# Layers 2 and 3 of a fused four-layer network: TensorE changes between them after every second pair of tiles

## The chip, the cores and the metric

The kernel runs on one core of a Trainium2 chip. The metric is the device time of one execution in microseconds (us), from the launch of the program on the core to its end. Five engines have instruction queues of their own: PE (TensorE, matrix multiplication), DVE (VectorE), ACT (ScalarE), POOL (GpSimd) and SP (SyncE, here only a queue that issues DMAs). PE writes its results to PSUM; DVE and ACT move them from there to SBUF, which is called an eviction below.

## The reference, cut to what matters

The input x is (4, 8, 512, 512) in f32; its first axis is called t below (0 to 3). Four layers follow, each of the form x = x + layer(gn(x)), where gn normalises every group of two channels over the whole image. Layer 0 is an attention with spiking neurons, layer 1 a 13 x 13 convolution of each channel. The change touches layers 2 and 3, two 3 x 3 convolutions over the 8 channels:

```python
def layer2(x):                       # x already normalised
    sx, sw = 127 / max(abs(x)), 127 / max(abs(weight))
    qx, qw = clip(round(x * sx)), clip(round(weight * sw))
    return conv3x3(qx, qw) / (sx * sw) + bias
def layer3(x):
    return conv3x3(x, weight) + bias
x = x + layer2(gn(x))
x = x + layer3(gn(x))                # this is the output
```

Layer 3 of one t can't start before the statistics of that t after layer 2 are known, since gn needs the mean and the variance of the whole image.

## The kernel before, in words

Layers 0 and 1 run first and leave x in DRAM, one tensor `x2` for each t. Function `layers23` then runs layers 2 and 3 in one loop.

**Tiles and pairs.** The 512 rows of an image are cut into 85 windows of 8 rows, each 6 rows after the last. A window has 8 rows x 8 channels = 64 partitions, so a tile of 128 partitions holds two windows, and two tiles make a pair. Each t has 22 pairs (`N_PAIRS`); the last of them holds a single window. A convolution is a matrix product with a banded matrix over the partitions, done three times with shifted columns. Layer 2 multiplies a whole tile by a 128 x 128 matrix in bf16, three matmuls for a tile, six for a pair (line L1118). Layer 3 works in f32 on each window alone, in one of four 64 x 64 quarters of the array, four quarters at a time: 24 matmuls for a pair (L1221).

**One turn of the loop.** Turn n issues layer 2 of pair n, counted over all t, and layer 3 of the pair 25 turns behind (22 pairs of a t and `LAG` = 3). In the order of the program it does this:

- `load` of pair n+5: two DMAs on SP bring x from DRAM into a tile of the pool `early["x"]` (L1068). The pool has 9 such tiles.
- `normalise` of pair n+2: ACT writes y (L1085; pool of 2). `quantise` of pair n+1: DVE rounds y to bf16 into one of three buffers xq (L1097), and POOL copies its two border columns (L1101, L1102).
- `layer2` of pair n: for each of its two tiles three matmuls on PE into a PSUM tile of the pool `ps_2`, called ps_q, which has 3; then DVE's eviction (L1125), which adds x and writes the sum into the ring `x3` in SBUF. For the statistics either ACT squares the tile and sums it (L1132) or DVE takes bn_stats (L1137).
- `halos`: where windows overlap, DMAs copy rows between neighbours in the ring (L1276), on SP's queue for t = 0 and on POOL's afterwards.
- `layer3` of pair n-25: POOL writes the border columns (L1214), PE multiplies into two PSUM tiles of `ps_3` (called ps_r, 4 tiles), ACT evicts them to o (L1230, pool of 10), and SP issues two DMAs to the output (L1237).
- Two steps of `norm3`, a generator that starts after the last pair of a t and computes its mean, variance and scaled band matrix. It is a chain of short DVE instructions (L1172 to L1203 and L178 to L197) with two small matmuls of line L181, the first for the mean and the second for the variance, and one of line L1199.

So turns 0 to 24 have layer 2 alone, turns 25 to 87 both layers, and turns 88 to 112 layer 3 alone. The first of a t's pairs has index 0, 22, 44 or 66.

**What sets the order.** Each engine runs its queue in order. The queues are laid out before the run by a scheduler that follows the order of the program and the dependences, and may move an instruction ahead of others where it expects time. `tc.issue_after(op)` keeps a block's instructions behind `op` on the same engine. PSUM tiles, tiles of x and the ring are reused in turn, and an instruction that writes a reused one waits for its last reader.

The ring `x3` has `RING` = 26 places of a pair. Pair n takes the place of pair n-26, whose layer 3 was issued in turn n-1. The lines that the change touches are these:

```python
HALF = P // 2
LAG = 3
RING = 23 + LAG
...
        "x": ctx.enter_context(pool("x2", 9, side="right")),
...
        if n >= N_PAIRS + LAG:
            t, p = divmod(n - N_PAIRS - LAG, N_PAIRS)
            with tc.issue_after(did):
                behind = (layer3(t, p, *norms[t]),)
```

## Time and profile before

| what | value |
|---|---|
| median of 3 runs | 2920.96 us (2919.23 to 2924.84) |
| profiled execution, its own time | 2921.53 us |
| its span, first to last instruction | 2919.3 us |
| TensorE clock granted, mean | 0.990 |
| layers 2 and 3, from about 2514 us to the end | 405 us |
| of these, both layers together | 2588 to 2849 us |
| PE busy over the span | 2819.7 us (97%) |
| DVE, ACT, POOL busy over the span | 2208.5, 551.0, 888.1 us |

The profile records one execution. A row of its views gives a source line, an engine, an operation, the tensors written and read, how often, and a time; times in the timeline count from the start of the span. In brackets stands how long the engine was idle before and what ended the wait. L1118 is line 1118 of the kernel before. The chain of waits is followed back from the last instruction to whatever released it each time; a line on it is on the path that sets the end.

### The profile page before, as it was taken

Reading aid. Unit: us, or ns where it says so; the run is one execution under the profiler, and the core shown is the slowest. Engines: PE = TensorE matmul, PEld = TensorE weight load, DVE = VectorE, ACT = ScalarE, POOL = GpSimd, SP = SyncE. Lnnn points to the kernel's source line nnn. Section 1 sums busy time; section 2 is a strip of 40 time slices with the busy share of each in tenths; the row PEclk is TensorE's granted clock in tenths of the full one; section 3 lists DMA queues with packets and bytes.
Section 4 is the critical chain, followed back from the end, with each engine's and each line's share of the span. In section 5 each row is a group of like instructions: output and inputs, shape, how many; then the busy total and the mean of one; then the engine's idle time right before and its main releaser. Section 6 shows DMA issues by size and latency. Waiting matters only on the chain. (4 is left out here: it accounts for less than half of the span.)

```text
span 2919.3 us, 36593 instructions
## 1 busy us (share of the span) xinstructions
PE 2819.7 (97%) x12865; PEld 1301.8 (45%) x12865; DVE 2208.5 (76%) x3916; ACT 551.0 (19%) x860; POOL 888.1 (30%) x1928
## 2 busy tenths in 40 slices
PE   6899999999999999999999999999999999679999
PEld 3454455554555554455455555545333333223334
DVE  7898688688779868877886886796665566888870
ACT  1300010010010001001000100110111121677774
POOL 3243233334224333323432343332311111232220
PEclk9899999999999999999999999999999999999999
DMA  7332322222322222222222111112877778699975
GB/s 180 96 81 78 79 62 63 70 70 77 73 59 66 69 75 74 69 59 67 69 70 59 45 52 52 52 52 62 226 202 207 201 212 220 170 199 238 219 193 147
DMA packets 323895, 322.10 MB, mean 110 GB/s; under 512 B 21431, under 2 KB 237183, under 8 KB 323599
## 3 DMA queue, kind: packets, MB, share of 16 engines
q1 hardware_dynamic: 261872, 237.39, 33.4%
q0 software_dynamic: 19776, 56.14, 6.0%
q10 hardware_dynamic: 42063, 26.23, 3.2%
q8 instruction: 101, 1.65, 0.3%
q14 instruction: 83, 0.68, 0.1%
HBM read 210.57 MB, written 103.60 MB: 108 GB/s over the span
## 5 line engine op out<-in xcount | busy, mean ns | idle before, releaser
L499 PE MATMUL ps_in<-w_v,xn 128*128 128x512 f32 x1024 | 459.5, 599 | 3.0 <-DVE xn L480 3.0
L499 PE MATMUL ps_in<-w_kq,xn 128*128 128x512 f32 x1024 | 450.1, 592 | 0.0
L815 PE MATMUL ps_conv<-x,bt 112*64 112x512 f32 x2048 | 445.2, 592 | 0.8 <-DVE v_p L467 0.8
L499 PE MATMUL ps_in<-xn,w_kq 128*128 128x512 f32 x1024 | 444.6, 592 | 0.0
L535 PE MATMUL ps_b<-toep,vtok 128*64 128x512 bf16 x3072 | 368.2, 383 | 1.0 <-DVE v_o L550 1.0
L450 ACT ACTIVATE h_q<-v_q,c_half 128x512 f32<-128x512 f32 x96 | 69.2, 721 | 1473.1 <-DVE v_q L446 852.3
L475 POOL TENSOR_TENSOR h_v<-h_v,c_v 128x512 f32<-128x512 f32 x96 | 121.9, 1270 | 686.0 <-DVE h_v L474 660.0
L584 POOL COPY x1s<-x1s 128x2 f32<-128x2 f32 (+1 forms) x1024 | 227.7, 277 | 273.3 <-DVE x1s L573 273.3
L562 PE MATMUL ps_out<-wp,so 128*128 128x512 f32 x1024 | 308.9, 444 | 0.0
L499 PEld LDWEIGHTS ps_in<-xn,w_kq 128*128 128x128 f32 x1024 | 194.3, 190 | 233.0 <-issue 222.0
L499 PEld LDWEIGHTS ps_in<-w_kq,xn 128*128 128x128 f32 x1024 | 194.2, 190 | 219.9 <-issue 205.0
L499 PEld LDWEIGHTS ps_in<-w_v,xn 128*128 128x128 f32 x1024 | 191.0, 191 | 218.5 <-issue 210.2
L815 PEld LDWEIGHTS ps_conv<-x,bt 112*64 112x64 f32 x2048 | 146.4, 135 | 288.9 <-issue 286.5
L535 PEld LDWEIGHTS <-vtok 128*64 128x64 bf16 x3072 | 175.6, 111 | 154.7 <-issue 5.6
L1221 PE MATMUL ps_conv<-x,band_t 64*64 64x512 f32 x2040 | 242.6, 595 | 0.0
L562 PEld LDWEIGHTS ps_out<-wp,so 128*128 128x128 f32 x1024 | 192.6, 188 | 94.4 <-issue 57.8
L1125 DVE SCALAR_TENSOR_TENSOR x<-ps_conv,inv,x 128x512 f32<-128x512 f32 (+1 forms) x172 | 187.4, 1185 | 45.7 <-PE ps_conv L1118 45.6
L573 DVE SCALAR_TENSOR_TENSOR x1s<-v_p,xr 128x256 f32<-128x256 f32 x256 | 188.5, 776 | 14.9 <-DMA x<-x1s 4.1
L837 POOL DMA_DIRECT2D x<-xo x128 | 71.6, 566 | 330.8 <-ACT xo L822 316.4
L822 ACT ACTIVATE xo<-ps_conv,off 128x512 f32<-128x512 f32 x128 | 87.8, 688 | 431.1 <-PE ps_conv L815 310.2
L475 POOL TENSOR_TENSOR h_k<-h_k,c_k 128x512 f32<-128x512 f32 x96 | 123.2, 1284 | 134.0 <-DVE h_k L474 134.0
L1118 PE MATMUL ps_conv<-xq,band 128*128 128x512 bf16 (+1 forms) x516 | 132.2, 393 | 30.3 <-POOL xq L1101 30.3
(193 smaller groups left out, 3161.4 us busy)
## 6 DMA issues: line engine op xcount, KB each, us to landing
x<-x SPq DMA_DIRECT2D x64, 917.0 KB
x<-x SPq DMA_DIRECT2D x168, 256.0 KB
x<-x1s POOLq DMA_DIRECT2D x128, 262.0 KB, 2.6
xq<-in_x SPq DMA_DIRECT2D x128, 256.0 KB
xr<-in_x SPq DMA_DIRECT2D x128, 256.0 KB
out<-o SPq DMA_DIRECT2D x164, 192.0 KB
xs<-in_x SPq DMA_DIRECT2D x112, 256.0 KB
x<-xo ACTq DMA_DIRECT2D x128, 128.0 KB
```

The source lines that it names most:

```text
L475: nc.gpsimd.tensor_add(h, h, c_twice[n])
L499: mm = nc.tensor.matmul(ps, lhsT=lhsT, rhs=rhs, start=k == 0, stop=k == NC - 1)
L535: nc.tensor.matmul(pb[two * DH : (two + 1) * DH, :], lhsT=v[:, c, h * DH : (h + 1) * DH], rhs=toep[z][:, h, u : u + N], start=c == 0 and z ...
L562: nc.tensor.matmul(ps, lhsT=so[:, k, c * P : (c + 1) * P], rhs=wpT[z][:, k, :], start=k == 0 and z == 0, stop=k == NC - 1 and z == 1,)
L573: nc.vector.scalar_tensor_tensor(own, v.rearrange("p (g v) -> p g v", g=PH)[:, two, :], 1.0, by_phase[:, two, :], op0=ALU.is_ge, op1=ALU.add,)
L584: nc.gpsimd.tensor_copy(x1[:, f, u : u + n], x1[:, fm, um - n + 1 : um + 1][:, ::-1])
L815: mm = nc.tensor.matmul(ps[q * M1 : (q + 1) * M1, :], lhsT=bt[:, z, :], rhs=xt[:, w0 : w0 + N_PS1, z : z + NV], start=z == 0, stop=z == SH ...
L822: nc.scalar.activation(xo[:, a, :], ps, AF.Identity, bias=off[:, t : t + 1])
L837: engine.dma_start(bass.AP(dst.tensor, dst.offset + (q * n_half * W1_OUT * B + b) * D + f * NV, [[B * D, W1_OUT], [W1_OUT * B * D, n_half] ...
L1118: mm = nc.tensor.matmul(ps[:n_p, :], lhsT=w["band2"][:n_p, j, dx, :n_p], rhs=xq[:, j, dx : dx + PH, :], start=dx == 0, stop=dx == 2,)
L1125: done["DVE"] = nc.vector.scalar_tensor_tensor(own.rearrange("p (v g) -> p g v", g=PH), by_phase(ps[:n_p, :]), w["inv"][:n_p], by_phase(x[ ...
L1221: mm = nc.tensor.matmul(ps[j][b * HALF : (b + 1) * HALF, :], lhsT=band[half, b, dx, :], rhs=x3[half, s0 + j, dx : dx + D], start=dx == 0, ...
```

## The change

Layer 3 is no longer issued in every turn. Its pairs are collected in the list `due`, and in turns with an odd n, and in every turn after the last of layer 2, all that is due is issued. So an even turn issues layer 2 of one pair and no layer 3, and an odd turn issues layer 2 of one pair and then layer 3 of two. Turn 25 still issues one.

Since layer 3 of a pair may come one turn later, the ring gets one more place, 27. A place holds 2 x 514 f32 numbers in each partition (4112 bytes), a tile of the pool of x 2 x 512 (4096 bytes); the pool of x goes from 9 tiles to 8.

```diff
-RING = 23 + LAG
+RING = 24 + LAG
...
-        "x": ctx.enter_context(pool("x2", 9, side="right")),
+        "x": ctx.enter_context(pool("x2", 8, side="right")),
...
-    norms, norm, done, behind = {}, iter(()), {}, ()
+    norms, norm, done, behind, due = {}, iter(()), {}, (), []
...
         if n >= N_PAIRS + LAG:
-            t, p = divmod(n - N_PAIRS - LAG, N_PAIRS)
+            due.append(divmod(n - N_PAIRS - LAG, N_PAIRS))
+        if due and (n % 2 or n >= n_all):
             with tc.issue_after(did):
-                behind = (layer3(t, p, *norms[t]),)
+                for t, p in due:
+                    behind = (layer3(t, p, *norms[t]),)
+            due = []
```

## The prediction

> **What bounds the kernel now.** I read the table by stage first, to see which engine fills each stretch of layers 2 and 3, then the chain of waits for what ends last, then the order of time around one turn. The stretches here are a mixed one (layers 2 and 3 together) and the tail (layer 3 alone); the columns are length, busy time of PE, weight loads, DVE, ACT and POOL, then PE clock, DMA share and GB/s.

> ```profile
> 2688.80:2745.00 56.20, 56.20 (x415) 18.01 (x414) 45.03 (x70) 41.69 (x70) 15.80 (x42) 1.00 0.92 245
> 2858.00:2910.00 52.00, 52.00 (x492) 27.41 (x488) 0.16 (x1) 27.84 (x41) 1.16 (x9) 1.00 0.54 159
> ```

> PE is never idle in either; DVE is at 80%, ACT 74%, DMA 92% in the mixed stretch. The chain agrees (start, length, what):

> ```profile
> 2692.96 2.74 PE ps_conv L1221 x24
> 2695.70 1.40 PE ps_conv L1118 x6
> 2697.09 2.74 PE ps_conv L1221 x24
> ...
> 2749.48 0.77 PE ps_conv L1118 x3
> ```

> A turn costs 1.40 + 2.74 = 4.14 us, all PE. How much of it is matmul? Three matmuls of L1118 end in 0.77 and six in 1.40, so one more costs 0.21. In the tail, where L1221 runs alone, ACT's evictions of a pair follow each other at 2898.52, 2901.09, 2903.67: 2.57 us for the same 24 matmuls. These run four at a time, so a step is 2.57/6 = 0.43[...]. Pure work is 6 x 0.214 + 2.57 = 3.86. The other **0.28 us is the two switches** between the layers: about 0.11 from 2 to 3, and 2.74 - 2.57 = 0.17 back.

> ```profile
> 2898.52 1.51 ACT L1230 ACTIVATE o<-ps_conv,const 128x512 f32<-128x512 f32 x2 [1.06 <-PE ps_conv L1221]
> 2901.09 1.51 ACT L1230 ACTIVATE o<-ps_conv,const 128x512 f32<-128x512 f32 x2 [1.06 <-PE ps_conv L1221]
> ```

> Where t changes, DVE is the bound for six turns: it also does norm3 there, and PE waits for it (timeline of PE):

> ```profile
> 2664.70 1.47 PE L1118 MATMUL ps_conv<-xq,band 128*128 128x512 bf16 x6
> 2666.83 0.38 PE L181 MATMUL gps_x<-gsum_x,avg_same 128*128 128x1 f32 x2 [0.66 <-DVE gsum_x L178]
> 2667.14 2.81 PE L1221 MATMUL ps_conv<-x,band_t 64*64 64x512 f32 x24
> 2669.88 1.47 PE L1118 MATMUL ps_conv<-xq,band 128*128 128x512 bf16 x6
> 2671.59 0.38 PE L181 MATMUL gps_x<-gsum_x,avg_same 128*128 128x1 f32 x2 [0.24 <-DVE gsum_x L178]
> ```

> Between the two L181 (the mean, then the variance) lies a pair of layer 3, which covers DVE's chain from one to the other: PE waits 0.66 + 0.24 only.

> [...]

> **The change part by part.**

> *Switches.* Turns 25 to 87 hold both layers: 63 times there and back now. Afterwards turn 25, then the odd turns 27 to 87: 32. The built program's order shows it (layer 2 of an even turn and an odd one, then two pairs of layer 3). At most 31 x 0.28 = 8.7 us go.

> *A new wait for PSUM.* Two pairs of layer 2 on end need four tiles, and ps_q has three. In the trace layer 2 begins at 2703.90 and DVE's first eviction at 2704.76, 0.86 later:

> ```profile
> 2703.90 1.47 PE L1118 MATMUL ps_conv<-xq,band 128*128 128x512 bf16 x6
> ...
> 2704.76 2.14 DVE L1125 SCALAR_TENSOR_TENSOR x<-ps_conv,inv,x 128x512 f32<-128x512 f32 x2 [0.86 <-PE ps_conv L1118]
> ```

> One eviction takes about 1.15 (1.109 is the least, 1.177 the mean of the group in 2700 to 2750). With 0.05 to hand over (gsum_x ends 2576.35, PE starts 2576.40) the bank is free at 0.86 + 1.15 + 0.05 = 2.06; PE wants it after three tiles, 3 x 0.643 = 1.93. It waits **0.13**, with all of layer 3 queued behind. Two turns become 2.06 + 0.64 + 0.11 + 5.14 + 0.17 = 8.13, instead of 8.28: 0.15 gained. The bounds are no wait (DVE's evictions start 0.99 apart; gain 0.28) and a wait that eats the switch (gain 0). Undisturbed doubles are turns 28 to 41, 48 to 63, 70 to 85: 7 + 8 + 8 = 23. **-3.4 us** (0 to -6.5).

> *DVE, ACT and POOL within a double.* DVE needs 2 x 3.27 (2704.76 to 2708.03, next idle) = 6.5 of 8.1. The odd turn's quantise ends near 7.4 and POOL's two copies (0.4 each) near 8.3; PE asks at 9.4: covered. ACT now does square, y, square, y, then four o: it resumes with square 2 near 6.3 and is done near 10.9, where the next square is just due; the next pair of layer 3 needs its banks at 10.8, and they were freed at 9.7. Cost 0, with some 1 us of cover.

> *The start.* Turn 27's layer 2 now follows turn 26's at once. Its quantise starts at 2592.14 and the first POOL copy ends at 2593.36 in the trace; PE would be free at 2591.00 + 1.29 = 2592.29. It waits 1.1, and gets back the 0.28 of a switch: **+0.8**.

> *Where t changes (turns 42 to 47 and 64 to 69).* Now 2657.36 to 2683.21 = 25.85 us. In the new order only layer 2 of turn 45 lies between the mean's L181 and the next layer 3, and the variance's L181 sits late in that pair. On DVE gsum_x now stands behind both evictions, bn_stats and the quantise of turn 45. Laid out from turn 42 (0): PE 1.29 + 0.64 + 0.11 + 5.14 + 0.17 reaches turn 44 at 7.35. DVE evicts 42 from 0.86, and with one more eviction and the norm's first part (2661.43 to 2663.42 is 1.99, 2665.79 to 2666.69 is 0.90) is free for turn 44 near 9.1. Two evictions 1.97, bn_stats 0.61, mean 0.1, quantise 0.6, two more evictions 1.97, bn_stats 0.61, quantise 0.6 and the five short norm steps (about 1.1) put gsum_x at 16.7. PE stands at that L181 from 13.2: **a wait of about 3.5 instead of 0.9**. Then 0.3 + 3.1 + 0.17 to turn 46, two pairs of layer 2 with the last norm matmul 3.0, layer 3 5.25 and 0.17: turn 48 near 28.7. Each of the two costs 2.8: **+5.6**. Bounds 1.5 each (the short steps fully overlapped, evictions 0.97) and 4 each[...].

> *The end.* Turns 86 and 87 keep their L181 wait (0.36) and save one switch: **-0.3**.

> *Queues and pools.* SP issues four output DMAs, then four loads, instead of two and two: 8 per 8.1 us as before. A load waits for its tile of x to be evicted, eight pairs back instead of nine: issued near 14 within the double, needed past 30. In turns 0 to 22 it loses one turn of lead (2.6 us) out of six; near 2547 SP is held up to 1.3 us by it, while the load issued at 2558.13 lands 8.91 later, 3.8 before its y. Cost 0, up to 1.3. POOL's halo DMAs keep their number but for the ring's wrap. The ring of 27 keeps the reuse one turn behind layer 3, as now: 0. Layers 0 and 1 are untouched.

> *Sum.* -3.4 + 0.8 + 5.6 - 0.3 = **+2.7** on the profiled execution's 2921.53. That execution is 0.6 above the median of the runs, 2920.96; against the median: 2923.7 us.

> **Rivals.** *Full gain:* all 31 switches go and nothing waits: -8.7, 2912.3. For it: PE is the only full engine between the changes of t. Against: three banks, and DVE's order at the changes of t. *The PSUM wait eats the gain:* if DVE begins an eviction later than 0.86, or a stopped PE restarts slowly, the fourth tile waits 0.28 or more; from there the doubles give nothing, and the start and the changes of t stand: +6.1, 2927; at 0.4 per double it is 2930. For it: DVE has 20% to spare only. Against: DVE is idle 0.86 before each first eviction now. *DMA:* the share is 0.92 to 0.95 already, and bunched output could make loads late; 257 GB/s were moved in 2596.6 to 2655, and 8.13 us need 1.96 MB, 241 GB/s, so I expect none; each us lost per double would cost 23. *It does nothing:* excluded by the built order.

> **Numbers.** A measurement of this kernel tells about 0.2% (5.8 us) from no change. Likeliest case, within that, 0.60; it holds the lost half of the switches and the longer norm wait in every size named above. Slower, by the PSUM wait or the DMA queue, 0.28. Faster, the full gain, 0.12. Range: 2917.5 (no PSUM wait and 1.5 per change of t: -3.1 - 2.6 from the sum, less a little) to 2931 (no gain in the doubles, 4 per change of t, 1.3 of late loads).

> **What would show it.** Right: L1118 in runs of 12 and L1221 in runs of 48; doubles of about 8.13 us, with a small wait of L1118 for DVE's L1125; one wait of 3 to 4 us at each of the two variance L181; 28 to 29 us over turns 42 to 47. Wrong: doubles of 8.0 without a wait, or of 8.28 and more; no long L181 wait; ACT or PE waiting for DMA in the mixed stretch.

## The result, and the profile after

| | before | after |
|---|---|---|
| median of 6 runs each | 2920.98 us (2919.23 to 2924.84) | 2936.81 us (2930.61 to 2939.81) |
| profiled execution, its own time | 2921.53 us | 2934.12 us |
| its span | 2919.3 us | 2932.3 us |

The ratio is 1.0051, with a 95% interval of 1.0041 to 1.0061: the change costs 12 to 18 us. The forecast of 2923.7 us, with a range up to 2931.0, was wrong. The runs of after also lie wider apart (9.2 us) than those of before (5.6).

Most of what was forecast is in the profile. A *double* is an even turn and the odd turn after it: two pairs of layer 2, then two of layer 3. In the table by stage (columns as in the prediction), the mixed stretch and the tail are as full as before:

```profile
2702.70:2759.60 56.90, 56.87 (x424) 19.76 (x420) 45.08 (x70) 41.74 (x68) 14.45 (x36) 1.00 0.89 217
2870.00:2922.00 52.00, 52.00 (x491) 20.53 (x488) 0.00 (x0) 27.06 (x40) 0.00 (x0) 1.00 0.51 150
```

In the chain of waits of after, L1118 comes in runs of 12 and L1221 in runs of 48, and one double follows the other at 2710.93 and 2719.07, 8.14 us apart. The timeline has their starts 8.13 apart (2710.87 and 2719.00), the forecast to the last digit; two turns cost 8.28 before.

```profile
2710.93 2.82 PE ps_conv L1118 x12
2713.75 5.32 PE ps_conv L1221 x48
2719.07 2.80 PE ps_conv L1118 x12
```

Where t changes, the timeline of PE has the forecast's one long wait, at the variance's L181:

```profile
2674.49 2.79 PE L1221 MATMUL ps_conv<-x,band_t 64*64 64x512 f32 x18
2679.95 0.38 PE L181 MATMUL gps_x<-gsum_x,avg_same 128*128 128x1 f32 x2 [2.68 <-DVE gsum_x L178]
2680.27 3.66 PE L1221 MATMUL ps_conv<-x,band_t 64*64 64x512 f32 x30
```

It is 2.68 us where 3.5 was laid out, and turns 42 to 47 take 27.82 us (2664.34 to 2692.16) where 28.7 was laid out.

What was not forecast stands in the view of waits. These are PE's waits from 2585 to 2905 us by line (us in total, times, longest), first before, then after:

```profile
PE gps_x L181 <- DVE gsum_x L178: 2.1, 5, 0.7
PE ps_conv L1118 <- POOL xq L1101: 1.4, 1, 1.4
```

```profile
PE ps_conv L1118 <- POOL xq L1101: 6.8, 4, 3.9
PE gps_x L181 <- DVE gsum_x L178: 5.3, 2, 2.7
PE ps_conv L1221 <- POOL x L1214: 4.5, 2, 2.3
```

The middle line is the forecast's change of t. The other two are waits for **POOL**. Of these the prediction had only the 1.0 us at turn 27, and 1.5 at turn 25 are in before too; 3.92 fall at turn 28, and 4.5 are waits for border copies.

**The first wait, at turn 28.** The timeline of PE:

```profile
2596.55 5.38 PE L1221 MATMUL ps_conv<-x,band_t 64*64 64x512 f32 x48
2605.86 4.44 PE L1118 MATMUL ps_conv<-xq,band 128*128 128x512 bf16 x12 [3.92 <-POOL xq L1101]
```

Layer 2 of turn 28 waits 3.92 us for the copies into xq. POOL's own timeline says why:

```profile
2595.39 1.16 POOL L1214 COPY x<-zero 128x4 f32<-128x4 f32 x9
2599.70 0.30 POOL L1214 COPY x<-zero 128x4 f32<-128x4 f32 x2 [3.16 <-DMA x<-x]
2603.61 1.27 POOL L1214 COPY x<-zero 128x4 f32<-128x4 f32 x10 [3.61 <-DMA x<-x]
...
2605.40 0.41 POOL L1101 COPY xq<-xq 128x254 bf16<-128x254 bf16 x1
```

All 21 border copies that were left of t = 0 stand in one block ahead of the copies into xq. Most of them are needed many turns later, but two of them wait for halos (L1276, written x<-x) to land, 3.16 and 3.61 us, and POOL runs its queue in order. POOL issued these two halos itself, at 2585.52 and 2591.97, and they landed 14.1 and 11.5 us later (in before 13.0 and 8.1). In before the 21 are spread between the copies into xq of several turns; of the two of them that wait for halos only one does so for long, and PE does not wait behind it at turn 28 (layer 2 starts at 2599.28, right behind layer 3). There was nothing to spare, though: that layer 2 takes 1.63 us in place of 1.47, with POOL's L1102 for it ending at 2599.82. POOL in before:

```profile
2593.64 1.04 POOL L1214 COPY x<-zero 128x4 f32<-128x4 f32 x8
2596.92 0.19 POOL L1214 COPY x<-zero 128x4 f32<-128x4 f32 x1 [2.25 <-DMA x<-x]
```

**The second kind, at turns 49 and 71.** Here the block of the new t, 21 copies, stands behind copies into xq that wait 4.12 us for DVE, and layer 3 of turn 49 waits 2.27 us for its first border copy (PE starts at 2697.36):

```profile
2696.43 0.40 POOL L1101 COPY xq<-xq 128x254 bf16<-128x254 bf16 x1 [4.12 <-DVE xq L1097]
2696.78 0.40 POOL L1102 COPY xq<-xq 128x254 bf16<-128x254 bf16 x1
2697.12 3.12 POOL L1214 COPY x<-zero 128x4 f32<-128x4 f32 x21
```

In before they come in smaller lots. The one that layer 3 of turn 48 (2684.61) needs stands first in a lot of ten, 0.7 us ahead of it, and PE does not wait:

```profile
2679.89 0.19 POOL L1214 COPY x<-zero 128x4 f32<-128x4 f32 x1
2683.87 1.27 POOL L1214 COPY x<-zero 128x4 f32<-128x4 f32 x10
```

**Behind the first wait, the clock.** The twelve matmuls of turn 28 take 4.44 us above and 2.88 in an undisturbed double. The table by stage has PE busy all the time, and PEclk, the third column from the end, at 0.58:

```profile
2602.00:2606.00 4.00, 0.14 (x1) 0.10 (x1) 0.00 (x0) 2.69 (x5) 2.39 (x13) 1.00 0.94 261
2606.00:2610.00 4.00, 4.00 (x12) 1.32 (x10) 3.25 (x5) 0.87 (x3) 3.59 (x8) 0.58 0.88 183
```

In steps of 0.25 us the clock is at one half from 2606.50 to 2610.25, which costs 1.7 us of full clock. Before has no such stretch from turn 25 to the end of its matmuls.

**The account** of the 13.0 us of span, from the starts of layer 2 in both profiles (the lag of after behind before). Turn 0 starts 1.6 later (2514.13 to 2515.72); layers 0 and 1 are unchanged, and over all the profiles of this study turn 0 starts anywhere from 2509.8 to 2516.3. At turn 42 the lag is 7.0 (2657.36 to 2664.34), though the doubles have given back 1.0; at turn 48 it is 9.0, at turn 50, behind the second kind of wait, 11.2 (2691.49 to 2702.67). The second change of t repeats it: 10.3 at turn 64, 12.1 at turn 70, 14.3 at turn 72 (2783.61 to 2797.93). Doubles and the end bring it back to 13.0. The median of after lies another 2.7 us above this execution. The other five have no trace; their mean granted clock, 0.988 or 0.989 against 0.990 here, fits more half clock.

### The profile page after: what moved, and what is told of

It reads as the page before. It is cut to its first block, busy times and chain, and to the rows that moved or that the text cites. A ratio compares the mean times of both kernels' runs of the same rounds, so it can differ in the third digit from the quotient of the medians.

```text
span 2932.3 us, 36586 instructions
## 1 busy us (share of the span) xinstructions
PE 2818.4 (96%) x12865; PEld 1302.4 (44%) x12865; DVE 2202.5 (75%) x3916; ACT 551.9 (19%) x860; POOL 885.1 (30%) x1926
## 5 line engine op out<-in xcount | busy, mean ns | idle before, releaser
L1221 PE MATMUL ps_conv<-x,band_t 64*64 64x512 f32 x2040 | 237.6, 592 | 4.5 <-POOL x L1214 4.5
L1125 DVE SCALAR_TENSOR_TENSOR x<-ps_conv,inv,x 128x512 f32<-128x512 f32 (+1 forms) x172 | 186.4, 1161 | 60.1 <-PE ps_conv L1118 51.6
L822 ACT ACTIVATE xo<-ps_conv,off 128x512 f32<-128x512 f32 x128 | 87.7, 687 | 431.4 <-PE ps_conv L815 299.8
L1118 PE MATMUL ps_conv<-xq,band 128*128 128x512 bf16 (+1 forms) x516 | 132.0, 396 | 35.4 <-POOL xq L1101 35.4
```

The source lines that it names most:

```text
L822: nc.scalar.activation(xo[:, a, :], ps, AF.Identity, bias=off[:, t : t + 1])
L1118: mm = nc.tensor.matmul(ps[:n_p, :], lhsT=w["band2"][:n_p, j, dx, :n_p], rhs=xq[:, j, dx : dx + PH, :], start=dx == 0, stop=dx == 2,)
L1125: done["DVE"] = nc.vector.scalar_tensor_tensor(own.rearrange("p (v g) -> p g v", g=PH), by_phase(ps[:n_p, :]), w["inv"][:n_p], by_phase(x[ ...
L1221: mm = nc.tensor.matmul(ps[j][b * HALF : (b + 1) * HALF, :], lhsT=band[half, b, dx, :], rhs=x3[half, s0 + j, dx : dx + D], start=dx == 0, ...
```

## The experiments

Three theories were put against each other. **A, POOL's queue:** the order of border copies and copies into xq on POOL, and what each of them waits for, makes PE late. **B, the grouping:** two pairs of layer 3 on end make DVE and ACT late, and the waits for POOL are only where that shows. **C, the memory:** with eight tiles of x the loads come late everywhere. After the first four runs the half clock came in as a second part of A. Each experiment ran beside before; ratios are to the runs of before in the same set, whose medians are 2919.94 (e1 to e4), 2919.28 (e5 to e8), 2919.71 (e9 to e12) and 2920.54 us (e13, e14).

| run | median, us | ratio, 95% interval | PE waits over 1.1 us behind turn 27, us | half clock in the profile, us of full clock lost behind turn 26 |
|---|---|---|---|---|
| e1 ring alone | 2927.99 | 1.0025, 1.0016 to 1.0034 | 6.23 | 3.4 |
| e2 pinned | 3009.05 | 1.0308, 1.0295 to 1.0321 | 29 times 2.0 to 2.3 (from turn 25); at L181 up to 5.8 | 20.5 |
| e3 pinned, single | 2991.79 | 1.0245, 1.0232 to 1.0258 | 23 times 2.2 to 2.3 (from turn 25); at L181 up to 4.5 | 15.4 |
| e4 grouping alone | 2935.82 | 1.0049, 1.0035 to 1.0063 | 1.30; 2.69, 2.67; 2.27, 2.31 | 12.0 |
| e5 early borders | 2922.58 | 1.0011, 1.0005 to 1.0018 | 2.67 and 2.66 | 5.1 |
| e6 early, L181 later | 2919.72 | 1.0002, 0.9994 to 1.0010 | 2.69 and 2.69 | 0 |
| e7 grouping, PE kept busy | 2929.43 | 1.0037, 1.0025 to 1.0050 | 2.30 and 2.33 | 1.7 |
| e8 before, early borders | 2919.43 | 1.0001, 0.9992 to 1.0009 | none | 0 |
| e9 early, single | 2917.06 | 0.9995, 0.9987 to 1.0003 | none | 0 |
| e10 eight x alone | 2922.57 | 1.0009, 1.0002 to 1.0016 | 1.15 | 0 |
| e11 e9 with before's memory | 2925.73 | 1.0023, 1.0015 to 1.0032 | 3.29 and 3.30 | 3.4 |
| e12 after again | 2934.71 | 1.0051, 1.0038 to 1.0064 | 4.24; 2.72, 2.77; 2.28, 2.28 | 3.4 |
| e13 memory, early borders | 2921.22 | 1.0002, 0.9993 to 1.0010 | none | 0 |
| e14 e9 again | 2917.59 | 0.9990, 0.9984 to 0.9997 | none | 0 |

### The parts alone: e1, e4, e10

e1 is before with the two numbers of the memory changed, and single turns (layer 3 of one pair in every turn, as before):

```diff
-RING = 23 + LAG
+RING = 24 + LAG
...
-        "x": ctx.enter_context(pool("x2", 9, side="right")),
+        "x": ctx.enter_context(pool("x2", 8, side="right")),
```

> The ring of 27 places and the eight tiles of x without the grouping: layer 3 of one pair in every turn, as before. Theory A (POOL's queue: the border copies L1214 stand in one block, behind transfers of halos that have not landed, ahead of the copies into xq L1101/L1102): this kernel's POOL order has the block of t = 0 as the kernel after has it, so the stall of layer 2 around turn 28 is there without any grouping, +3 to +6 us, about 2924 to 2927 us; the doubles stay at 8.28 us a two-turn step and the changes of t at 25.85 us. Theory B (the grouping itself makes TensorE late): no difference from before, 2921 us. Theory C (with eight tiles of x the loads come late): waits for L1068's loads spread over all turns, +7 us or more, none of it at one place.

Measured: 2927.99 us, 8.1 over before. The timeline of PE has the whole of it at one place, with no grouping in the program:

```profile
2593.31 2.81 PE L1221 MATMUL ps_conv<-x,band_t 64*64 64x512 f32 x24
2602.34 2.72 PE L1118 MATMUL ps_conv<-xq,band 128*128 128x512 bf16 x6 [6.23 <-POOL xq L1101]
```

POOL waits 3.61 and 4.65 us there for halos, in the same block of L1214, and the clock is at one half from 2599.50 to 2606.50. The sum came out a little over A's 3 to 6 us, the place as expected, and the two turns cost 8.28 elsewhere. So the first wait comes from the memory part and needs no grouping. C's spread-out waits are not there. Why the scheduler lays the copies out in one block when the ring has 27 places is not shown.

e4 is the grouping with the memory of before. Layer 3 comes one turn earlier, so that 26 places do:

```diff
-        if n >= N_PAIRS + LAG:
-            due.append(divmod(n - N_PAIRS - LAG, N_PAIRS))
+        if n >= N_PAIRS + LAG - 1:
+            due.append(divmod(n - N_PAIRS - LAG + 1, N_PAIRS))
```

> The grouping without the memory: a ring of 26 places, nine tiles of x, and layer 3 one turn earlier (pair n-24 and n-25 at every odd turn n), so that two pairs fit. Its POOL order has the border copies of t = 0 spread much as before. Theory A: no stall of 4 us at turn 28, at most 1 to 2 us there; the changes of t cost +2 to +3 us each and may have their own wait for L1214; doubles 8.13 us: 2922 to 2928 us. Theory B: as after, 2934 to 2938 us. Theory C: all but the doubles as before, 2919 to 2922 us.

Measured: 2935.82 us, but from 2924.30 to 2940.74. At turn 28 the wait is 1.30, as A expected, and the waits of the grouping are there twice each: 2.69 and 2.67 at L181, 2.27 and 2.31 for L1214, as in after. The median is where B expected it; one run of the six is in A's range. In the profiled execution the difference is the clock: 12.0 us of the 2940.74. The six runs' mean granted clock goes the same way: 0.991 in the run of 2924.30, 0.987 to 0.989 in the four near 2935, 0.985 in that of 2940.74. In the table by stage, around the wait at the first change of t:

```profile
2675.00:2678.00 3.00, 0.34 (x2) 0.34 (x2) 2.60 (x8) 1.21 (x3) 0.00 (x0) 0.82 1.00 96
2678.00:2681.00 3.00, 3.00 (x10) 1.11 (x10) 1.16 (x3) 1.56 (x3) 2.43 (x6) 0.50 0.96 341
2681.00:2684.00 3.00, 3.00 (x4) 0.70 (x4) 0.00 (x0) 0.44 (x1) 0.00 (x0) 0.50 0.90 260
```

PE is busy throughout from 2678 and has half its clock until 2687.25: 10.5 us at one half, 5.1 lost, and the same again at the second change of t. The profile of after has a wait of the same length at the same place, 2.68, and full clock behind it. The record shows what differs. In each profile the clock changes only on a grid of 3.413 us, and a wait can fall into one window of it or be split over two. Here are the windows of that grid around the two waits, first e4, then after (the first number behind the comma is PE's busy time, the third from the end the clock):

```profile
2673.48:2676.89 3.41, 1.49 (x10) 0.27 (x2) 3.41 (x11) 0.98 (x2) 0.74 (x2) 1.00 1.09 88
2676.89:2680.30 3.41, 2.64 (x9) 1.25 (x10) 1.87 (x5) 1.97 (x4) 1.77 (x5) 0.50 0.95 269
```

```profile
2674.91:2678.32 3.41, 2.36 (x18) 0.57 (x10) 3.41 (x9) 1.76 (x3) 0.74 (x2) 1.00 1.12 116
2678.32:2681.74 3.42, 1.79 (x18) 0.94 (x22) 2.25 (x8) 2.31 (x4) 1.12 (x3) 1.00 1.02 155
```

In e4 1.92 us of the wait fall into one window, and the next is at half clock. In after the wait is split into 1.05 and 1.63, and the clock stays. Where a window begins differs from one execution to the next (in e12, the same kernel as after, the grid lies 0.75 us earlier in the span), which fits the scatter of the runs.

e10 splits the memory part: before with eight tiles of x, and the order on POOL unchanged.

> The kernel before with eight tiles of x instead of nine, and nothing else; the order on POOL is that of before. Theory A: nothing, 2918 to 2921 us, so that what the ring and the eight tiles cost together (e1) is the ring's. Theory C (late loads): +7 us as in e1.

Measured: 2922.57 us, 2.9 over before (0.6 to 4.7 by the interval): not nothing, and not C's 7. The timeline of POOL shows that it goes the same way:

```profile
2596.42 0.19 POOL L1214 COPY x<-zero 128x4 f32<-128x4 f32 x1 [3.08 <-DMA x<-x]
...
2600.66 0.19 POOL L1214 COPY x<-zero 128x4 f32<-128x4 f32 x1 [1.24 <-DMA x<-x]
```

The one wait of 2.25 in before has become 3.08 and 1.24, and PE waits 1.15 and 1.03 for xq behind them. Why the two halos land later with eight tiles (13.8 and 11.5 us from issue) is open: SP's waits for DMAs of loads in 2540 to 2600 grew only from 5.7 to 8.7 us. Since the block of 21 is in e1 and not here, the eight tiles alone do not make it; it takes the ring of 27.

### POOL's order mended: e2, e3, e5, e8, e13

e2 was a clumsy mend: the border copies of a turn's layer 3 stand behind the copies into xq of the same turn.

```diff
-            with tc.issue_after(did):
+            with tc.issue_after(did), tc.issue_after(done["POOL"]):
```

> The kernel after with the order on POOL pinned: the border copies of a turn's layer 3 stand behind the copies into xq of that turn. Theory A: the wait of 3.92 us before layer 2 of turn 28 and what follows it (some 6 us in all) and the two waits of 2.27 us for L1214 go; some 9 us of the 13 come back, 2926 to 2929 us. What stays is the wait for the variance at the two changes of t (+2.0 each) and what the doubles save (about -2 to -3.4). Theory B or C: the same time as after, 2934 to 2938 us, the waits for POOL turned into others.

Measured: 3009.05 us, 80 over what A expected. The wait at turn 28 is gone, but the view of waits of PE has a new one in nearly every double:

```profile
PE ps_conv L1223 <- POOL x L1214: 61.1, 27, 2.3
```

In a double the quantise of the odd turn ends late on DVE (7.4 us into it by the prediction's own layout); the copies into xq follow it, and the border copy now had to follow them, 2.3 us after PE wanted it. Twenty-nine such waits make 65.7 us and the half clock 20.5; the waits at L181, 14.9 us against 2.1 in before, come on top, and the doubles give some back. The span is 87.7 us over before's. So e2 says nothing between A and B, but shows how sharp the place on POOL is. e3 is e2 with single turns at the changes of t, and has the same fault.

> As the pinned kernel, and layer 3 of one pair a turn in turns 42 to 49 and 64 to 71, so that the two changes of t go as in the kernel before. Theory A with the prediction's price of the change of t: the waits for the variance fall to those of before, -2.0 us each, less 2 x 4 x 0.15 us of doubles that become single turns: about 2.7 us under the pinned kernel, 2923 to 2926 us; if the +1.6 us before layer 2 is chance, 2920 to 2922 us. If the price of the change of t is not the wait for the variance, the same as the pinned kernel.

Measured: 2991.79 us; 23 waits, 52.5 us.

e5 is the mend proper. The border copies become a function of their own, called ahead of their layer 3, so that one stands behind each turn's copies into xq:

```diff
+        with tc.issue_after(done["POOL"]):
+            while bordered < n_all and bordered <= n + 2 - N_PAIRS - LAG and bordered // N_PAIRS in norms:
+                borders(*divmod(bordered, N_PAIRS))
+                bordered += 1
```

> The kernel after with the border copies L1214 issued up to two turns ahead of their layer 3, one behind each turn's copies into xq and ahead of the next turn's. Theory A (POOL's queue): the wait of 3.92 us before layer 2 of turn 28, the half clock behind it (1.7) and the two waits of 2.27 us for L1214 go, about -10 us: 2922 to 2928 us; the waits of 2.7 us for the variance (L181) stay, and in some runs the half clock behind them, so the runs still scatter by some us. Theory B (the grouping itself): 2934 to 2938 us with the waits somewhere else.

Measured: 2922.58 us, in A's range. By the ratios, 1.0051 and 1.0011, some 12 of the 15 us are back. PE's waits in the same stretch as above:

```profile
PE gps_x L181 <- DVE gsum_x L178: 5.3, 2, 2.7
PE ps_conv L1118 <- POOL xq L1101: 1.0, 1, 1.0
```

The first is the change of t, the second the forecast's 1.1 at turn 27. The waits for POOL that were not forecast are gone, none has taken their place, and the grouping is all there. So B falls, but for the two waits at the changes of t, which are the grouping's own and were forecast (5.1 us of half clock follow them in this profile). e8 is the control, the same mend on before.

> Control: the kernel before with its border copies issued early in the same way. Theory A: before loses next to nothing to POOL's order, so no difference, 2918 to 2921 us; if POOL's order were worth much by itself (so that e5's gain says nothing of the change), 2915 us or less.

Measured: 2919.43 us, no difference. What e5 brings is the repair of what the change broke, not a gain that before could have had. e13 does the same for the memory part:

> The memory part of the change (ring of 27, eight tiles of x) with early borders and layer 3 of one pair in every turn: what e9 is without its doubles. If the ring and the eight tiles cost nothing once POOL's order is mended: 2918 to 2921 us, and the doubles of e14 are worth the prediction's 2.7 us against it. If eight tiles of x cost their 2.9 us of e10 here too: 2921 to 2924 us, and the doubles are worth over 5 us.

Measured: 2921.22 us, ratio 1.0002. The 7 us of e1, and the 2.9 of e10 within them, are gone with the order on POOL: the ring and the eight tiles have no cost of their own over some 3 us, the end of the interval. In e13 the two halos land as late as in after, 15.4 and 12.5 us from issue, so it was the order behind them that cost time and not the landing.

### The changes of t and the clock: e6, e7, e9, e11, e12, e14

e6 holds the variance's L181 of turns 45 and 67 back until the first pair of layer 3 is through.

> As the kernel with early borders, and the variance's L181 of turns 45 and 67 stands between the two pairs of layer 3 instead of ahead of them. Theory A with the clock as second cause: no wait of TensorE over 1 us is left in turns 28 to 87, so no half clock either; the change of t costs two more switches (0.3) instead of 2.0. From the prediction's sum: -3.4 (doubles) + 0.8 (start) + 0.6 - 0.3 = -2.3 against before: 2916 to 2920 us, and the runs lie as close as those of before (5 us). If the wait for the variance returns at the next matmul (L1199 or the next double), 2922 to 2926 us.

Measured: 2919.72 us, in the range, but not for the reason given: the wait is still there, 2.69. The scheduler of after had already moved this L181 into the first pair, behind 18 of its 24 matmuls; e6 moves it by six. From turn 44 to turn 46 layer 2 advances in 11.37 us (2663.23 to 2674.60) instead of 13.89 in e5 (1.7 of these half clock). The median is 2.9 us under e5: about 0.8 at this change of t, as much at the other if it goes alike, and the rest would be half clock, which e6's profile does not have.

e7 tests the clock by itself, on e4: eleven matmuls ahead of that L181.

> The grouping alone (ring of 26, nine tiles of x, as e4) with eleven matmuls of 128x512 bf16 into an unused bank ahead of the variance's L181, whose result nobody reads: TensorE works for about 2.4 of the 2.7 us that it waited there. They add no work that TensorE would have time for anything else in. Clock theory (a wait of TensorE over 2 us can halve its granted clock for 3.4, 6.8 or 10.2 us): no half clock at turns 45 and 67, up to 5.1 us less at each, median 2925 to 2930 us and a profile with clock 1.00 there. If the half clock has nothing to do with the wait: 2934 to 2938 us as e4.

Measured: 2929.43 us, 2928.47 to 2932.95, in the range expected of the clock theory. Its median is 6.4 under e4's, but the two are from different sets and the intervals of their ratios overlap (1.0025 to 1.0050, 1.0035 to 1.0063). Nor does it isolate the clock. The added matmuls waited 0.70 for the bank of the mean and L181 still waited 2.30, so that the wait was cut in two and not filled; layer 3, now kept behind L181, lost both its waits for L1214 (4.6 us); and half clock of 1.7 followed at one of the changes. The half clock in the profile fell from 12.0 to 1.7, but with so much moved at once e7 only agrees with the clock following the waits. Which waits it followed is counted by the windows of the grid, in the next section.

e9 is e5 with single turns around the changes of t:

```diff
-        if due and (n % 2 or n >= n_all):
+        if due and (n % 2 or n >= n_all or n in SINGLE):
```

`SINGLE` holds the turns 42 to 49 and 64 to 71.

> The kernel after with early borders (as e5) and layer 3 of one pair a turn in turns 42 to 49 and 64 to 71, so that the two changes of t go as before. If the prediction's other terms hold: doubles -0.15 x 21 = -3.2, start +0.8, end -0.3, changes of t 0: 2.7 us under before, 2916 to 2918 us, with no wait over 1 us and no half clock after turn 28, so runs as close as before's. If the doubles save nothing (the PSUM wait eats it): 2919 to 2921 us.

Measured: 2917.06 us, as expected. PE's waits from 2585 on, all that is left:

```profile
PE gps_x L181 <- DVE gsum_x L178: 1.9, 4, 0.8
PE ps_conv L1118 <- POOL xq L1101: 0.9, 1, 0.9
```

e11 tried the same with the memory of before.

> As e9 with the memory of before: a ring of 26 places, nine tiles of x, layer 3 one turn earlier. Same working as e9: 2916 to 2918 us. If layer 3 one turn earlier meets its halos (L1276) before they have landed: a wait of POOL at L1213 with the copies into xq behind it, 2920 to 2925 us.

Measured: 2925.73 us, slower, by neither of the expected ways. Layer 3 one turn earlier meets the scaled band matrix of the new t: PE waits 3.29 us for DVE's L1190 at turn 46 and again at 68, with 1.7 of half clock behind each. In e9, with layer 3 one turn later, that wait is not there: this turn of lead, for which the ring of 27 has room, is what lets the first pair of a t go without it.

e12 is after once more.

> The kernel after once more, for a second profile. POOL's two kinds of waits are in the built order, so they return at the same turns: about 3.9 us before layer 2 of turn 28 and 2.3 us before layer 3 of turns 49 and 71. The half clock[...] may follow other waits this time: 2930 to 2940 us, and the difference between this profile's span and the first one's lies in the half clock and in layers 0 and 1.

Measured: 2934.71 us, ratio 1.0051 again. The waits are the same ones at the same turns: 4.24, then 2.72 and 2.28, then 2.77 and 2.28. The half clock is 3.4 this time, all of it behind turn 28. The span is shorter than the first one's (2928.4 to 2932.3) because turn 0 starts 5.0 us earlier, and 1.7 more of half clock takes part of that back.

e14 repeats e9 beside e13.

> e9 once more, beside e13 on the same chip: 2916 to 2918 us; 2.7 us under e13 if the prediction's sum for the doubles, the start and the end is right, 5 us or more under it if the eight tiles cost e13 something.

Measured: 2917.59 us, 3.6 under e13, whose memory and POOL order it has. Its ratio to before, 0.9990 with an interval of 0.9984 to 0.9997, makes it the one measurement here whose whole interval lies under before, by 1 to 5 us. The same kernel's first measurement, e9, had 0.9987 to 1.0003, which takes in no difference; so the gain is small and barely clear.

## Why the prediction was wrong

**Switches and the PSUM wait: right.** 8.13 us for a double, as worked out, and all of the gain's lost half goes to the fourth tile: in the chain of after a double's L1118 is cut 2.05 + 0.03 of issue + 0.81 where its fourth tile begins, 2.08 into it where 2.06 was laid out. In the double that starts at 2710.87 DVE's first eviction ends at 2712.89 and the fourth tile begins at 2712.95. The 2.05 us are nine matmuls, a tile of the second pair among them, and 0.77 + 6 x 0.21 is 2.03, so there is no gap between the two pairs of layer 2. What a switch does within PE is not shown; its 0.28 for both ways is the author's estimate from the turns and the tail of before. e14 against e13 gives the doubles, the start and the end together, with 21 doubles: -0.15 x 21 + 0.8 - 0.3 = -2.7 by the prediction, -3.6 by the medians.

**Start: right for turn 27** (1.02 us of wait, 1.1 laid out), and the end too (turn 86 to the end of the span, 77.76 to 77.41). The step on the start stopped one turn too soon, since turn 28 is where POOL is late.

**Changes of t: right in mechanism, too large in size.** +1.97 and +1.87 (27.80 us from 2759.67, against 25.93) where +2.8 each was taken, within the bounds of 1.5 and 4. e9 against e5 shows the two changes of t and the half clock behind them worth 5.5 us by the medians and 4.7 by the ratios.

**"Queues and pools", the step that failed.** It priced late loads ("Cost 0, up to 1.3"), and of POOL it said only that the halo DMAs "keep their number but for the ring's wrap"; the step on the inside of a double had called POOL's two copies into xq covered. So POOL's border copies, and what they hold up, stood at nothing. Measured in the profile: 3.92 at turn 28, 2.27 twice, and 1.7 of half clock, 10.2 us. With this in the sum, and with the changes of t at their size, the sum is 2.7 + 10.2 - 1.8 = 11.1, and with the 1.6 of layers 0 and 1 it is 12.7, against 13.0 measured. The error was one of method. The step counted POOL's DMAs and did not follow the order of its queue, though the built order of after, from which the prediction took its number of switches, has the block of border copies ahead of the copies into xq. In before the 2.25 us wait of L1214 for a DMA was to be seen as well, with PE's layer 2 already 0.16 us longer behind it: a wait of this kind in a queue that feeds PE is a risk to be priced.

**The range** ended at 2931.0. It took in each bound of the listed terms, but nothing for the order of a queue. The chance of slower, 0.28, was placed on the PSUM wait and the DMA queue, and neither happened: undisturbed doubles have no further wait, and by e13 the loads cost nothing that could be measured. DMAs came in elsewhere, by the halos that POOL waited for.

## What to carry to other kernels

When a change moves work in a program that a scheduler lays out, read the built order of every queue that feeds the full engine, not the counts: look there for instructions that wait for a DMA and have nothing urgent behind their own result, and see what urgent work stands behind them. Price a new wait of PE of 2 us or more with the clock as well, 0 to 5 us on top in these profiles. And a gain of 0.15 us a step needs its few bad places (here turns 28, 45, 49, 67 and 71) mended before it shows.

## What the runs showed of the hardware

Waits of TensorE cost time after their end in these runs: behind waits of 2.3 to 6.2 us the granted clock was, in some cases, one half for one, two or three windows of 3.413 us in the midst of full work, 1.7, 3.4 or 5.1 us lost. What told the cases apart was PE's busy time within one window of a fixed grid of 3.413 us: under 1.4 us was followed by half clock in 20 of 20 windows, over 1.75 us in none of 1482. So of 69 waits of 2.0 to 2.8 us from 2588 us on 17 were followed by half clock, by where they fell, and all nine of 3.3 us or more. This is counted from the profiles; no experiment moved a wait against the grid. The two halo DMAs that POOL's border copies waited for near turn 28 (176 and 160 KB) took 8.1 to 15.4 us from issue to landing (before 13.0 and 8.1, with a DMA share of 0.99 and 0.88 meanwhile; after 14.1 and 11.5, with 1.05 and 1.00; e13 15.4 and 12.5). Without any change to their code, layers 0 and 1 end up to 6.6 us apart from one profile to the next (turn 0 from 2509.75 to 2516.32), as much as the effects studied here.
